# A graph network on one core: where the last stores are issued, and the order inside some neighbour groups

## The chip, the cores and the metric

The kernel runs on one core of one Trainium2 chip. A core has five engines that run side by side and meet at semaphores: TensorE (PE, matrix products; its weight loads are listed as PEld), VectorE (DVE), ScalarE (ACT), GpSimd (POOL) and SyncE (SP, which here only issues transfers). SBUF holds the working data, PSUM takes what PE writes. Transfers (DMAs) are issued from the queues of SP, ACT and POOL.

The metric is the device time of one execution in microseconds. Three runs of the kernel before gave 1960.7, 1963.19 and 1964.54; the median is 1963.19.

## The reference

There are 128 graphs of 128 nodes with 256 features, all float32, and an adjacency matrix for each. Two layers follow each other, both with a layer norm, a ReLU and a residual:

```
h = relu(layernorm(x))
s = h @ w_se.T + b_se                          # three features per node
A = exp(-|s_n - s_m|^2) * adj                  # distances, masked
msg = relu(h @ w_msg.T + b_msg)
x_nmp = A @ msg                                # the neighbours' messages
x_conv = relu(h + bn2(conv17(relu(bn1(conv1(h))))))   # along the nodes
x = x + gru([x_conv, x_nmp], h)                # gates r, z and n

h = relu(layernorm(x))                         # second layer: nodes 0..24 only
for g in five groups of nodes:
    h1 = relu(normadj_g @ (h_g @ W1[g]) + b1[g])
    fused[:, nodes of g] += softmax(w)[g] * relu(normadj_g @ (h1 @ W2[g]) + b2[g])
x = x + fused
```

## The kernel before, in words

**Tiling.** Four graphs make a group (`GB = 4`), so there are 32 groups, numbered 0 to 31. The convolution of 17 taps is done by a Fourier transform of 80 points, in two batches of 16 groups.

**Stages.** Layer A (`stage_a`) normalises, makes the first product and transforms. Layer B (`stage_b`) multiplies, for each of 40 frequencies, the transformed data by transformed weights, which POOL adds up beforehand (tiles `xs` and `wf`, L544 and L545). So the sequence is A, B for the first batch, A, B for the second. Then layer C (`stage_c`) transforms back and computes the gates for all groups, while the second layer (`rows`, `prepare`, `pair`) follows behind it for the nodes below 25.

**Neighbour groups.** Beside A, B and the start of C runs a lane of 32 programs, `early(q)`, one for each group. Each loads the group's data (two DMAs on SP, for the next group ahead), runs `neighbours`, and stores the result from POOL (`xmd`, L709). `neighbours` has these steps:
- pse: sixteen small matmuls (L647), four ACT instructions into `ef` (L651), one DVE product into `lr` (L654)
- two messages: for each, eight matmul instructions pm (L663), an addition of the bias on DVE (L666) and a ReLU on ACT (L668)
- the distances: a product of `lr` (L676) and a transpose of the adjacency (L678) for each graph into a tile `pd`, the exponential on ACT (L680) and the mask product on DVE (L681) into `aT`
- px, in two halves: messages times `aT` (L689), and a copy to `xm` on DVE (L691)

`pse`, `pm`, `pd` and `px` take turns in five PSUM buffers (pool `ptmp`).

**The order of the work.** The order in which instructions are given to each engine is fixed when the program is built, by a planner (`Order`, `Lane`). Each program is a generator that yields after a step a pair: what the step costs PE, and how long after it the next one should wait. The planner moves its own clock by the first number, and of the lanes whose next step is due it takes the one with the least work done by its weight. So `yield 0.9, 3.0` after the distances keeps px back by 3.0 of the planner's units unless there is nothing else to take. At the start of the first B the program waits 10 units, loads weights and waits 5 more; at the second B only 5; at the start of C a load waits 7 and another 6. In these times the neighbour lane is all that the planner has.

**The end.** `pair` of the last two blocks ends in the steps `turn`, `gather` and `fuse`. `fuse(h)` makes a weighted sum over the five groups of nodes for eight graphs (two matmuls of 512 columns, one for each half of the partitions), adds it to `x1` on DVE and stores it. Of the last block, h = 2 and h = 3, each graph has its own store of 32 KB: the eight of h = 2 all on SP, those of h = 3 on SP and ACT in turn.

Of the kernel before, what the change touches and what calls it, by code (L numbers as in the profile page):

```python
# [19 lines left out]
P = 128  # L20
GB = 4
# [189 lines left out]
def kernel(ctx: ExitStack, tc: tile.TileContext, x, adj, consts, vecs, w_se, conv1_w,  # L211
# [162 lines left out]
    brow = xf.tile([P, D], FP, name="brow")  # L374
    LATE, XA, MOM = {}, {}, {}
    A_DONE, B_DONE, G_DONE, C_DONE = set(), set(), {-1}, set()

    def take_turn(name, bufs, **kw):
        while turn:
            turn.pop().close()  # L380
        turn.append(ExitStack())
        LATE[name] = turn[-1].enter_context(
            tc.tile_pool(name=name, bufs=bufs, side="right", **kw))
# [142 lines left out]
    def stage_b(bat):  # L526
        while "wrz" not in LATE:
            yield 0.0, 0.5
        if bat == 0:
            yield 0.0, 10.0  # L530
        WF, xf = {}, LATE["xw"]

        def load_w(f):
            w = WF[f] = xf.tile([P, 2, 3, D], FP, tag="wf", name=f"wf{bat}_{f}", bufs=4)
            for k in range(2):
                nc.sync.dma_start(out=w[:, k, :2], in_=wfd[f::NF + 1, k * P:(k + 1) * P]
                                  .rearrange("s p o -> p s o"))

        XS = {}

        def add(f):

            XS[f] = xf.tile([P, 2, P], FP, tag="xs", name=f"xs{bat}_{f}", bufs=2)
            nc.gpsimd.tensor_tensor(XS[f], X[:, :, 2 * f], X[:, :, 2 * f + 1], ALU.add)  # L544
            nc.gpsimd.tensor_tensor(WF[f][:, :, 2], WF[f][:, :, 0], WF[f][:, :, 1], ALU.add)  # L545

        def product(ps, xk, f, s):

            for k in range(2):
                nc.tensor.matmul(ps, xk(k), WF[f][:, k, s], start=(k == 0), stop=(k == 1))  # L550

        for f in range(3):
            load_w(f)
        yield 0.0, 5.0
        late = None
        for f in range(NF + 1):
            if f + 3 <= NF:
                load_w(f + 3)
            if f < NF:
                add(f + 1)  # L560
            if f >= NF - 6 and f % 3 == 0 and bat + 1 < NBAT:
                n = (bat + 1) * BQ + (f - NF + 6) // 3
                XA[n] = LATE["xe"].tile([P, 4, D], FP, name=f"xa{n}")
                load_x(XA[n], n)
            n = (bat + 1) * BQ
            if f == NF - 3 and n in XA:
                MOM[n] = moments(XA[n], "a")
            if f == NF - 1 and n in XA:
                normalize(XA[n], XA[n], *MOM[n])
            y = xf.tile([P, 2, D], FP, tag="y", name=f"y{bat}_{f}")  # L570
            pa = pgat.tile([P, 2, D], FP, tag="gat", name=f"pa{bat}_{f}")
            for s in range(2):
                product(pa[:, s], lambda k: X[:, k, 2 * f + (s if f == 0 else 1 - s)], f, s)
            if f == 0:
                nc.vector.tensor_copy(y, pa)
            else:
                pb = ptmp.tile([P, D], FP, tag="tmp", name=f"pb{bat}_{f}")
                xs = XS.pop(f)
                product(pb, lambda k: xs[:, k], f, 2)
                kk = xf.tile([P, D], FP, tag="kk", name=f"kk{bat}_{f}", bufs=2)  # L580
                nc.scalar.activation(kk, pb, AF.Copy)  # L581
                nc.vector.scalar_tensor_tensor(y, pa, 2.0, kk[:, None].to_broadcast([P, 2, D]),  # L582
                                               op0=ALU.mult, op1=ALU.subtract)
            WF.pop(f)
            if late is not None:
                nc.gpsimd.dma_start(out=yd[bat][:, 2 * f - 2:2 * f], in_=late)
            late = y
            yield 1.7 if f == 0 else 2.6, 1.0
        nc.gpsimd.dma_start(out=yd[bat][:, F - 2:F], in_=late)
        B_DONE.add(bat)  # L590
# [49 lines left out]
    def neighbours(q, hT, ad, xm):  # L640


        bmsg = LATE["bmsg"] if q else bm0
        pse = ptmp.tile([P, 512], FP, tag="tmp", name=f"pse{q}")
        for k in range(2):
            for j in range(GB):
                nc.tensor.matmul(pse[j * WIDE:(j + 1) * WIDE, :N], wse9[:, k],  # L647
                                 hT[:, k, j * N:(j + 1) * N], start=(k == 0), stop=(k == 1))
        ef = LATE["fr"].tile([P, 4, N], FP, tag="ef", name=f"ef{q}")
        for i in range(4):  # L650
            nc.scalar.activation(ef[:, i], pse[:, :N], AF.Identity, scale=emb[:, i:i + 1],  # L651
                                 bias=embb[:, i:i + 1])
        lr = LATE["fr"].tile([P, 2, N], FP, tag="lr", name=f"lr{q}")
        nc.vector.tensor_tensor(lr, ef[:, 0::2], ef[:, 1::2], ALU.mult)  # L654
        yield 0.5, 0.0

        msgs = []
        for h in range(2):
            pm = ptmp.tile([P, 2, D], FP, tag="tmp", name=f"pm{q}_{h}")
            for i in range(2):  # L660
                j = 2 * h + i
                for k in range(2):
                    nc.tensor.matmul(pm[:, i], hT[:, k, j * N:(j + 1) * N], LATE["wmsg"][:, k],  # L663
                                     start=(k == 0), stop=(k == 1))
            msg = LATE["fr"].tile([P, 2, D], FP, tag=f"msg{h}", name=f"msg{q}_{h}")
            nc.vector.tensor_tensor(  # L666
                msg, pm, bmsg[:, None, :].to_broadcast([P, 2, D]), ALU.add)
            nc.scalar.activation(msg, msg, AF.Relu)  # L668
            msgs.append(msg)
            yield 1.75, 0.0  # L670

        pds = [ptmp.tile([P, 2, N], FP, tag="tmp", name=f"pd{q}_{j}") for j in range(GB)]
        aT = LATE["fr"].tile([P, GB, N], FP, tag="aT", name=f"aT{q}")
        for j in range(GB):
            rows = slice(j * WIDE, (j + 1) * WIDE)
            nc.tensor.matmul(pds[j][:, 0], lr[rows, 0], lr[rows, 1], start=True, stop=True)  # L676
        for j in range(GB):
            nc.tensor.transpose(pds[j][:, 1], ad[:, j], ident)  # L678
        for j in range(GB):
            nc.scalar.activation(aT[:, j], pds[j][:, 0], AF.Exp)  # L680
            nc.vector.tensor_mul(aT[:, j], aT[:, j], pds[j][:, 1])  # L681
        yield 0.9, 3.0


        for h in range(2):
            px = ptmp.tile([P, 2, 2, N], FP, tag="tmp", name=f"px{q}_{h}")
            for i in range(2):
                for dc in range(2):
                    nc.tensor.matmul(px[:, dc, i], msgs[h][:, i, dc * P:(dc + 1) * P],  # L689
                                     aT[:, 2 * h + i], start=True, stop=True)  # L690
            nc.vector.tensor_copy(xm[:, :, h * 256:(h + 1) * 256],  # L691
                                  px.rearrange("p d i n -> p d (i n)"))
            yield 0.9, 0.0
# [411 lines left out]
    def pair(pr):  # L1105
# [93 lines left out]
        def fuse(h):  # L1199
            zt, blk = hz[:, h % 3], b0 + h // 2  # L1200
            x1 = X1[blk][:, 2 * (h % 2):2 * (h % 2) + 2]
            pf = ptmp.tile([P, 2, D], FP, tag="tmp", name=f"pfu{pr}_{h}")
            for s in range(2):
                nc.tensor.matmul(pf[s * 2 * WIDE:(s + 1) * 2 * WIDE], s2w, zt[:, :, s],
                                 start=True, stop=True)
            nc.vector.tensor_add(x1, x1, pf)
            for i in range(2):
                g0 = (b0 * QS + 2 * h + i) * GB
                if blk < NBLK - 1:
                    nc.gpsimd.dma_start(out=out[g0:g0 + GB, :WIDE], in_=x1[:, i])  # L1210
                    continue
                for j in range(GB):
                    eng = nc.scalar if h % 2 and j % 2 else nc.sync
                    eng.dma_start(out=out[g0 + j, :WIDE], in_=x1[j * WIDE:(j + 1) * WIDE, i])

        tail = [(turn, 0), (turn, 1), (turn, 2), (turn, 3), (gather, 0), (turn, 4), (turn, 5),
# [25 lines left out]
    for bat, (during_a, during_b) in enumerate(((0.66, 0.5), (0.2, 0.65))):  # L1242
        if bat:
            take_turn("ab", 2, reuse_waits="tile")
        begin = Lane([stage_a(q) for q in range(bat * BQ, (bat + 1) * BQ)], ahead=3)
        beside.weight = during_a
        order.run(begin, beside, *[gates] * bat, until=begin)
        take_turn("xw", 3, reuse_waits="tile")
        products = Lane([stage_b(bat)])
        beside.weight = during_b  # L1250
        order.run(products, beside, *[gates] * bat, until=products)
    turn.pop().close()
    lab.close()
    LATE["co"] = ctx.enter_context(
# [52 lines left out]
```

## Time and profile before

| what | value |
|---|---|
| median of three runs | 1963.19 us |
| profiled execution, its own time | 1960.66 us |
| its span (first to last instruction) | 1958.9 us |
| mean granted clock of TensorE | 0.999 |
| share of the chain that ended last on PE | 83% |
| layer A and B with both batches | to about 657 us |
| neighbour groups | 161 to 801 us |
| layer C | from 671 us |
| last addition of the final sum | 1949.84 to 1950.53 us |

The profile comes from one execution. A row such as "177.43 2.05 PE L689 MATMUL px<-aT,msg ... x16 [0.97 <-DVE aT L681]" says that sixteen instructions of line 689 began at 177.43 us, took 2.05 us together, and that the engine had stood idle for 0.97 us before them until DVE wrote `aT`. The chain of waits is followed back from the last instruction: at each step to what released it.

### The profile page before, as it was taken

How to read it: one execution, taken by the hardware profiler on the slowest of the kernel's cores; microseconds unless marked ns; L12 is line 12 of the kernel's file. 1: busy time of each engine (PE TensorE's matmuls, PEld its weight loads, DVE VectorE, ACT ScalarE, POOL GpSimd, SP SyncE). 2: the span in 40 equal slices, each digit the busy share in tenths (PEclk: the TensorE clock that was granted, in tenths of full speed). 3: DMA queues.
4: the chain of work that ended last, by engine and by line, in shares of the span. 5: the costliest groups of instructions: out<-in, count | busy, mean ns of one | idle time of the engine just before them, and what ended most of it. 6: DMA issues, size and time to landing. Idle time of an engine off the chain costs nothing.

```text
span 1958.9 us, 32171 instructions
## 1 busy us (share of the span) xinstructions
PE 1925.5 (98%) x12048; PEld 1591.1 (81%) x12048; DVE 1341.2 (68%) x2965; ACT 670.8 (34%) x1504; POOL 656.7 (34%) x899
## 2 busy tenths in 40 slices
PE   9999999999999999999999999999999999999997
PEld 6668888889888888887888787888877788887865
DVE  6775445786443576796883886885788787588852
ACT  4664222445223334322223332232332223223233
POOL 3452666332565201332321333231133222114220
PEclk9999999999999999999999999999999999999999
DMA  9988878744778744633433344254344334334232
GB/s 217 308 276 271 272 252 286 218 142 172 251 255 260 213 114 132 188 95 84 112 95 97 96 108 112 79 134 97 92 115 101 89 101 112 100 90 120 63 70 68
DMA packets 180982, 296.66 MB, mean 151 GB/s; under 512 B 28326, under 2 KB 131947, under 8 KB 180571
## 3 DMA queue, kind: packets, MB, share of 16 engines
q1 hardware_dynamic: 134874, 162.20, 28.9%
q0 software_dynamic: 44800, 131.66, 23.8%
q8 instruction: 95, 1.56, 0.3%
q10 hardware_dynamic: 1152, 0.74, 0.1%
q14 instruction: 61, 0.49, 0.1%
HBM read 197.97 MB, written 109.05 MB: 157 GB/s over the span
## 4 chain that ended last, share of the span: by engine, by line
PE 83%; DVE 11%; DMA 2%; ACT 1%; issue 1%; SPq 1%; POOL 0%; DVEq 0%; ACTq 0%; POOLq 0%
PE p L776 37%; PE pa L550 7%; PE pm L663 5%; PE pz L1150 5%; PE ph L1138 5%; PE pc L429 4%; PE pb L550 3%; PE pf L444 3%; PE px L689 3%; PE pi L733 2%; PE pw L496 1%; DMA xa<-in_x 1%; PE ph L418 1%; PE py L1122 1%; DVE xc L742 1%
## 5 line engine op out<-in xcount | busy, mean ns | idle before, releaser
L958 POOL DMA_DIRECT2D x1d<-xt x128 | 101.2, 815 | 403.6 <-DVE xt L956 390.5
L582 DVE SCALAR_TENSOR_TENSOR y<-pa,kk 128x512 f32<-128x512 f32 x78 | 53.8, 690 | 151.4 <-ACT kk L581 151.4
L858 POOL DMA_DIRECT2D xt<-in_x x128 | 100.6, 793 | 161.3 <-DMA x1d<-xt 148.1
L550 PE MATMUL pa<-wf,X 128*128 128x256 f32 x640 | 152.2, 381 | 0.0
L776 PE MATMUL p<-th,wrz 128*128 128x256 f32 x512 | 134.2, 384 | 0.0
L776 PE MATMUL p<-tm,wrz 128*128 128x256 f32 x512 | 131.4, 379 | 0.0
L776 PE MATMUL p<-tc,wrz 128*128 128x256 f32 x512 | 131.4, 379 | 0.0
L550 PEld LDWEIGHTS pa<-wf,X 128*128 128x128 f32 x640 | 118.1, 190 | 16.2 <-issue 2.0
L429 PE MATMUL pc<-c1w,hTa 128*128 128x256 f32 x512 | 120.9, 382 | 2.8 <-DVE X L450 1.7
L663 PE MATMUL pm<-wmsg,hT 128*128 128x256 f32 x512 | 121.5, 382 | 0.0
L776 PEld LDWEIGHTS p<-th,wrz 128*128 128x128 f32 x512 | 94.7, 190 | 19.1 <-issue 6.6
L429 PEld LDWEIGHTS pc<-c1w,hTa 128*128 128x128 f32 x512 | 93.6, 190 | 20.1 <-DVE h L432 4.8
L776 PEld LDWEIGHTS p<-tc,wrz 128*128 128x128 f32 x512 | 97.2, 190 | 13.5 <-issue 0.5
L663 PEld LDWEIGHTS pm<-wmsg,hT 128*128 128x128 f32 x512 | 95.8, 190 | 15.2 <-ACT kk L581 1.4
L776 PEld LDWEIGHTS p<-tm,wrz 128*128 128x128 f32 x512 | 97.3, 190 | 13.2
L745 ACT ACTIVATE xc<-xc,t_bn 128x256 f32<-128x256 f32 x128 | 58.1, 501 | 145.3 <-DVE xc L742 145.3
L776 PE MATMUL p<-hTc,wrz 128*128 128x256 f32 x384 | 99.7, 382 | 1.3 <-DVE z L850 1.2
L776 PE MATMUL p<-xc,wrz 128*128 128x256 f32 x384 | 98.6, 379 | 0.0
L776 PE MATMUL p<-xm,wrz 128*128 128x256 f32 x384 | 98.5, 379 | 0.0
L545 POOL TENSOR_TENSOR wf<-wf 128x512 f32<-128x512 f32 x78 | 98.5, 1263 | 0.0
L1138 PE MATMUL ph<-yz,w 128*128 128x400 f32 (+3 forms) x448 | 96.6, 369 | 1.8 <-DVE yz L1125 1.8
L1150 PE MATMUL pz<-hz,w 128*128 128x400 f32 (+3 forms) x448 | 95.7, 368 | 0.5 <-DVE yz L1152 0.5
(213 smaller groups left out, 4329.5 us busy)
## 6 DMA issues: line engine op xcount, KB each, us to landing
wf<-wfd SPq DMA_DIRECT2D x160, 256.0 KB
wfd<-ws POOLq DMA_DIRECT2D x64, 320.0 KB, 9.3
yd<-y POOLq DMA_DIRECT2D x80, 256.0 KB, 4.4
yt<-yd SPq DMA_DIRECT2D x64, 320.0 KB
xa<-in_x SPq DMA_DIRECT2D x128, 128.0 KB
hTd<-hTa POOLq DMA_DIRECT2D x32, 512.0 KB, 6.5
hT<-hTd SPq DMA_DIRECT2D x32, 512.0 KB
xmd<-xnmp POOLq DMA_DIRECT2D x32, 512.0 KB, 6.0
```

The source lines that it names most:

```text
L429: nc.tensor.matmul(pc[:, i], hT[:, k, (2 * h + i) * N:(2 * h + i + 1) * N], c1w[:, k], start=(k == 0), stop=(k == 1))
L444: nc.tensor.matmul(pf[:, i, :F * NB], h1[:, 2 * h + i, k * P:(k + 1) * P], fwd, start=True, stop=True)
L545: nc.gpsimd.tensor_tensor(WF[f][:, :, 2], WF[f][:, :, 0], WF[f][:, :, 1], ALU.add)
L550: nc.tensor.matmul(ps, xk(k), WF[f][:, k, s], start=(k == 0), stop=(k == 1))
L663: nc.tensor.matmul(pm[:, i], hT[:, k, j * N:(j + 1) * N], LATE["wmsg"][:, k], start=(k == 0), stop=(k == 1))
L689: nc.tensor.matmul(px[:, dc, i], msgs[h][:, i, dc * P:(dc + 1) * P], aT[:, 2 * h + i], start=True, stop=True)
L745: nc.scalar.activation(xc[:, co, s], xc[:, co, s], AF.Relu, bias=sft["bn2"][:, co:co + 1])
L776: nc.tensor.matmul(ps[:, m], w[:, i, k, m * P:(m + 1) * P], factor(i, x, t), start=first and j == 0, stop=last and j == len(n) - 1, skip_g ...
L858: nc.gpsimd.dma_start(out=xt[a * WIDE:(a + 1) * WIDE].rearrange("p b d c -> p (b d) c"), in_=slices(x[q * GB:(q + 1) * GB])[a])
L958: nc.gpsimd.dma_start(out=slices(x1d[q])[a], in_=xt[a * WIDE:(a + 1) * WIDE].rearrange("p b d c -> p (b d) c"))
L1138: nc.tensor.matmul(ph, w1[:, k, m * P:(m + 1) * P], yz[:, k, s:s + nb, o:o + n], start=(k == 0), stop=(k == 1))
L1150: nc.tensor.matmul(pz, w2[:, g, m, cc * P:(cc + 1) * P], hs[i][:, m], start=(m == 0), stop=(m == 3))
```

## The change

There are two edits. In `neighbours` a flag, read after the first step, chooses between two orders. Where it is down the order is the old one. Where it is up, the distances are given out after the first message and before the second, with the transposes ahead of the products, and the step of its own (`yield 0.9, 3.0`) is left out, so that px follows the second message. The flag is set when a pass of layer A is finished, taken down at every frequency of layer B, and set again before layer C, where it stays up.

In `fuse` the stores and the sum of the last block are divided in another way. For h = 2 the first four graphs go out in one store on POOL; all other single stores alternate between SP and ACT. For h = 3 the sum is made in two halves of 256 columns, each with its own addition.

```diff
+    LONE = [False]
...
@@ stage_b @@
+            LONE[0] = False
             y = xf.tile([P, 2, D], FP, tag="y", name=f"y{bat}_{f}")
...
@@ neighbours @@
+        alone = LONE[0]
+
+        def distances():
+            pds = [ptmp.tile([P, 2, N], FP, tag="tmp", name=f"pd{q}_{j}") for j in range(GB)]
+            aT = LATE["fr"].tile([P, GB, N], FP, tag="aT", name=f"aT{q}")
+            if alone:
+                for j in range(GB):
+                    nc.tensor.transpose(pds[j][:, 1], ad[:, j], ident)
+            for j in range(GB):
+                rows = slice(j * WIDE, (j + 1) * WIDE)
+                nc.tensor.matmul(pds[j][:, 0], lr[rows, 0], lr[rows, 1], start=True, stop=True)
+            if not alone:
+                for j in range(GB):
+                    nc.tensor.transpose(pds[j][:, 1], ad[:, j], ident)
+            for j in range(GB):
+                nc.scalar.activation(aT[:, j], pds[j][:, 0], AF.Exp)
+                nc.vector.tensor_mul(aT[:, j], aT[:, j], pds[j][:, 1])
+            return aT
+
         msgs = []
         for h in range(2):
+            if alone and h:
+                aT = distances()
             pm = ptmp.tile([P, 2, D], FP, tag="tmp", name=f"pm{q}_{h}")
...
-        pds = [ptmp.tile([P, 2, N], FP, tag="tmp", name=f"pd{q}_{j}") for j in range(GB)]
...
-        yield 0.9, 3.0
+        if not alone:
+            aT = distances()
+            yield 0.9, 3.0
...
@@ fuse @@
-            for s in range(2):
-                nc.tensor.matmul(pf[s * 2 * WIDE:(s + 1) * 2 * WIDE], s2w, zt[:, :, s],
-                                 start=True, stop=True)
-            nc.vector.tensor_add(x1, x1, pf)
+            final = blk == NBLK - 1 and h % 2
+            for i in (slice(0, 2),) if not final else (slice(0, 1), slice(1, 2)):
+                for s in range(2):
+                    nc.tensor.matmul(pf[s * 2 * WIDE:(s + 1) * 2 * WIDE, i], s2w, zt[:, i, s],
+                                     start=True, stop=True)
+                nc.vector.tensor_add(x1[:, i], x1[:, i], pf[:, i])
             for i in range(2):
                 g0 = (b0 * QS + 2 * h + i) * GB
-                if blk < NBLK - 1:
+                if blk < NBLK - 1 or (i == 0 and not final):
                     nc.gpsimd.dma_start(out=out[g0:g0 + GB, :WIDE], in_=x1[:, i])
                     continue
                 for j in range(GB):
-                    eng = nc.scalar if h % 2 and j % 2 else nc.sync
+                    eng = nc.scalar if j % 2 else nc.sync
                     eng.dma_start(out=out[g0 + j, :WIDE], in_=x1[j * WIDE:(j + 1) * WIDE, i])
...
@@ tile_gnn_kernel @@
         order.run(begin, beside, *[gates] * bat, until=begin)
+        LONE[0] = True
         take_turn("xw", 3, reuse_waits="tile")
...
+    LONE[0] = True
     turn.pop().close()
```

## The prediction

> **What bounds the kernel now.** I read the page's busy times first, then the chain of waits, then the timeline of TensorE (PE) wherever PE stood still, and last the queues at the very end.
>
> ```profile
> PE 1925.5 (98%) x12048; PEld 1591.1 (81%) x12048; DVE 1341.2 (68%) x2965; ACT 670.8 (34%) x1504; POOL 656.7 (34%) x899
> ```
>
> PE is busy 1925.5 of 1958.9 us at a granted clock of 0.999. So 33 us in all can be won without taking matmuls away, and this change takes none away: it moves idle time of PE, and it moves the end of the span.
>
> The chain of waits shows the idle time that the first edit aims at (columns: start, us, what):
>
> ```profile
> 175.47 0.70 DVE msg L666
> ...
> 176.26 0.63 ACT msg L668
> 176.89 0.18 ACT aT L680
> ...
> 177.43 2.05 PE px L689 x16
> ```
>
> The second message's matmuls (pm) end at 175.45. After them its addition and ReLU, then the exponential and the mask product, stand between PE and px. The same groups on PE's timeline, with the other place of this kind at 663.77:
>
> ```profile
> 177.43 2.05 PE L689 MATMUL px<-aT,msg 128*128 128x128 f32 x16 [0.97 <-DVE aT L681]
> ...
> 183.54 1.89 PE L550 MATMUL pa<-wf,X 128*128 128x256 f32 x8
> ...
> 663.77 2.05 PE L689 MATMUL px<-aT,msg 128*128 128x128 f32 x16 [0.97 <-DVE aT L681]
> ```
>
> Two groups (1 and 25, by counting the pse rows) cost 0.97 us each. Group 2 stood before the first Fourier product too (183.54), but its distances fell behind that product and cost nothing. The timelines of VectorE (DVE) show what can hurt:
>
> ```profile
> 173.45 0.43 DVE L654 TENSOR_TENSOR lr<-ef 128x256 f32<-128x256 f32 x1 [1.51 <-ACT ef L651]
> ...
> 181.72 3.47 DVE L654 TENSOR_TENSOR lr<-ef 128x256 f32<-128x256 f32 x1 [1.51 <-ACT ef L651]
> ...
> 664.23 0.42 DVE L618 TENSOR_TENSOR th<-hTc 128x256 f32<-128x256 f32 x1
> ```
>
> The same lr took 0.43 us alone and 3.47 us while POOL ran its xs and wf sums (181.06 to 184.90). At the end, on the queue of SyncE (SP), with its row in the table of waits last:
>
> ```profile
> 1948.63 0.36 SPq L1214 DMA_DIRECT2D out<-x  x1
> ...
> 1953.34 0.31 SPq L1214 DMA_DIRECT2D out<-x  x1
> ...
> 1956.09 0.42 SPq L1214 DMA_DIRECT2D out<-x  x1
> ...
> SPq L1214 <- DMA out<-x: 1.6, 3, 1.2
> ```
>
> SP issues 12 of the 16 small stores, ACT four from 1950.56 on; three of SP's wait for the landing of an earlier store (1.6 us), the first from about 1952.1 to 1953.34, and the last starts at 1956.09. The span ends 2.8 us after that start.
>
> **The final stores.** Taken away: 12 issues on SP and 4 on ACT. Put in: one 128 KB store on POOL, six small ones each on SP and ACT. The last addition (0.69) starts at 1949.84, after four matmul instructions of 512 columns in 1.67 us. In halves there are eight of 256; PE must still wait for the second ReLU, so the first half can be added about 0.4 earlier and the last ends near 1950.25, for 1950.53. That 0.3 counts only if nothing later binds, and something does: the waits on landings say that from the ninth small store on a store needs an early one landed. With twelve stores, four instead of eight are behind that point. Taking the observed 1953.34 for the first of them, SP issues two in 0.46 steps, the last starts at 1953.8 and the end is 1953.8 + 2.8 = 1956.6: a gain of 2.3. If the early ones land at once, SP's last starts near 1951.2, but then the POOL store ends it: 1948.63 + 5.0 (median issue to landing of the four such stores, 4.1 to 5.9) = 1953.6, plus about 1.2 of closing work = 1954.8; a gain of 4.1. If the fifth POOL store delays the early small ones by 1.6 (a fifth of the 7.9 us from the first POOL store's issue at 1944.84 to the last one's landing, 1947.76 + 5.0), the gain is 0.7. POOL, ACT and SP have nothing else queued. I take 2.0, near the row.
>
> The Trainium skill, "DMA: Bandwidth & Descriptors", section "Issuing engines are not separate DMA queues", speaks against this part: more issuing engines save only the issuing time. By it the five or six issues that leave SP would be worth about 2.4 us (six by 0.4) and nothing of the landing waits; the rows above have those waits besides.
>
> **Which groups are alone.** The flag is read after a group's first step. It is up from the end of a layer A pass to the first product, and in all of layer C. By the planner's own costs a group shrinks from 6.7 plus 3.0 of delay to 5.8, so more fits into the 15 units (10 + 5, first pass), 5 (second) and about 13 (7 + 6, layer C) that pass before the main lane's first product. Ahead of the first product come all of groups 1 and 2 and half of group 3; ahead of the second, all of group 15; ahead of C, one whole group more. The work on PE is only put earlier. On SP the loads of group 3 now go before the first wf loads, which then start near 176.5 instead of 166.9; their product comes near 189, so 1.5 MB has about 12 us. On POOL group 2's store goes before the first sums; they are done about 3.5 us after group 2's px, and the product that reads them stands behind group 3's second message, about 7 us after it.
>
> **What an alone group costs.** PE: pse 0.57, pm 1.83, transposes and distances 1.1, pm 1.83, px. The exponentials and mask products are now under the second message: there the 0.97 goes. What is late next is that message: by the chain it is ready 1.5 us after its matmuls (175.45 to 176.89 and a hand-over), and the first half of px covers only 0.9. The second half of px waits about 0.6, with hand-overs 0.65. Nothing else can step between, since no other lane is ready, and everything behind on PE waits too.
>
> Sum over the places, in PE idle time:
> - First product: group 1, 0.65 for 0.97: -0.3. Group 2 had cover, now +0.65. Group 3's lr meets POOL's sums, and its distances are now asked for after one message and one product instead of after both messages: between 0 and 1.2, I take 0.9, by the 3.47 row. Together +1.25.
> - Second product: group 15 hid its distances behind two products, now +0.65 (0.5 to 1.0).
> - Layer C: 0.97 before; now two groups of 0.65, and the eight sums of C (L618, 664.23 to 667.24, 3.0 us of DVE) fall between a group's first message and its mask products or lr: 0 to 2.2, I take 1.2, in the middle, because the place depends on the planner's phase. Together +1.5 (-0.3 to +2.5).
> - Inside C: PE idles 2.0 us between 671 and 850 (179.00 less 176.99 in the table of windows), where five groups are woven in. Two of them now run earlier: 2/5 of it, -0.8. The ends: all 2.0 goes, or each of four groups pays 0.65 (+2.6).
> - End: -2.0 (-4.1 to -0.7).
>
> Sum: 1.25 + 0.65 + 1.5 - 0.8 - 2.0 = +0.6 us. The profiled execution took 1960.66 (span 1958.9 and 1.8 around it), 2.5 below the median 1963.19 of three runs; on the median the forecast is **1963.8**.
>
> For the lr row the Trainium skill, "SBUF — State Buffer", section "Who interferes with whom", has a VectorE operation with two SBUF inputs block fully until the reading GpSimd operation is done. By that rule as written lr would wait out one sum (at most 1.26 us, the longest POOL row there); the 3.47 row waited out the whole run of four, and with one sum group 3 would pay nothing and the total would be -0.3.
>
> **The rivals.** A difference of 0.2% (3.9 us: below 1959.3, above 1967.1) is about what a measurement of this kernel can tell from no change.
> - *Faster.* The second message hides: px waits only for hand-overs. Groups 1 and 25 give back 0.97 each, the three others pay 0.1 each, lr meets no sums, C gives 0.8, the end 2.0: -4.4, 1958.8; with the end's full 4.1 it is 1956.7. For it: the two 0.97 rows are exactly this pause. Against it: the 0.70 and 0.63 of msg in the chain, longer than half a px.
> - *Slower.* In C the alone groups pay at the second px, on a DVE that is 74% busy there (132.56 of 179.00), so that the message's addition queues: 1.0 (the longest wait of px on aT) by four groups, +4.0 in place of -0.8: +5.4, 1968.6. It decides from three such groups on. Against it: in C other matmuls can stand between the two halves of px, and did for group 27 to 30.
> - *The end does not move.* The fifth POOL store holds up the small ones, and the ring of landings still sets the end: -0.7 for -2.0, 1965.1. For it: the POOL stores' 5.0 us. It stays within 0.2%.
>
> **Chances.** Forecast 0.38, end not moving 0.12: within 0.2% 0.50. Faster 0.26, slower 0.24; the bounds of C and of the end make both sides possible. The likeliest case by itself spans 1961 to 1966; the range goes to the other cases, 1957.5 to 1968, leaving about 1 in 10 on each side.
>
> **What would show it.** Right: in groups 1 and 2 px splits into two halves with a wait of 0.6 between them, released by ACT's message, and no wait at the first half; group 2's px ahead of the first pa; 12 small stores and one more on POOL; the last small store starting near 1953.8. Wrong: px without a gap (faster), new gaps of px on msg or aT between 690 and 790 (slower), a last store after 1955 (end not moving). A layer C reordered so far that gaps past 850 change by more than 2 us would upset the whole sum.

## The result, and the profile after

The changed kernel takes 1975.72 us (median of six runs, 1972.73 to 1981.6). The kernel before, run beside it, takes 1962.19 (six runs, 1960.41 to 1965.22). The ratio is 1.0064, with a 95% interval of 1.0048 to 1.0081: **slower by 13.5 us**. The forecast was 1963.8, a rise of 0.6, and its range ended at 1968.

The profiled execution took 1979.52 us. Its span is 1977.7 us, 18.8 longer than the 1958.9 of before, and its granted clock is 0.994 for 0.999. The busy times from the page:

```profile
PE 1933.8 (98%) x12052; PEld 1599.9 (81%) x12052; DVE 1354.3 (68%) x2966; ACT 662.5 (34%) x1498; POOL 657.7 (33%) x900
```

PE does the same matrix work as before (the four instructions more are the halves of the last sum), yet it is busy 8.3 us longer. So the 18.8 us are two things: 8.3 of busy time and 10.6 of idle time. The busy time goes with the clock: in some stretches the profile shows a granted clock of 0.5, called half clock here. This table adds up PE's gaps by place. The last column is PE's busy time inside the stretches at half clock, halved, since that work would have taken half as long at full clock; without it PE is busy 1924.9 us, for 1925.5 before.

| place (time in the trace after) | idle before | idle after | difference | half clock adds |
|---|---|---|---|---|
| start, to the first neighbour group (0 to 165) | 6.05 | 9.51 | +3.5 | 2.6 |
| groups ahead of the first product (165 to 202) | 1.31 | 2.76 | +1.45 | 0 |
| second layer A pass (355 to 513) | 3.62 | 6.95 | +3.3 | 4.7 |
| groups ahead of the second product (513 to 530) | 0.00 | 2.93 | +2.9 | 0 |
| groups ahead of layer C (688 to 714) | 0.97 | 2.50 | +1.5 | 1.7 |
| layer C with groups woven in (714 to 839) | 2.01 | 2.33 | +0.3 | 0 |
| the rest, to the last matmul | 10.32 | 10.37 | +0.1 | 0 |
| last matmul to the end of the span | 9.08 | 6.54 | -2.5 | 0 |

The sum is 10.6 idle and about 9.0 at half clock, 19.6 for the 18.8 seen. The start runs the same instructions in both kernels, and its idle time lies between 4.0 and 11.0 us over the profiles of this study. Without its 6.1 us the table gives +13.5, which is the difference of the medians. That they agree so well is luck: the table compares one execution with one, and the execution of before has less half clock than most. Its granted clock is 0.999, where the executions of before that were timed beside the experiments have 0.994 to 0.999 and a median of 0.997.

**Ahead of the first product.** PE's timeline of after (start, us, instruction, and in brackets the idle time before it with its releaser):

```profile
180.41 1.05 PE L702 MATMUL px<-aT,msg 128*128 128x128 f32 x8
182.08 1.16 PE L702 MATMUL px<-aT,msg 128*128 128x128 f32 x8 [0.61 <-ACT msg L691]
...
190.06 1.16 PE L702 MATMUL px<-aT,msg 128*128 128x128 f32 x8 [0.61 <-ACT msg L691]
...
196.98 0.50 PE L669 MATMUL pd<-lr 32*128 32x128 f32 x8 [1.10 <-DVE lr L656]
```

The single pause of 0.97 ahead of px has gone. In its place px is split by 0.61 in groups 1 and 2, and group 3's distances wait 1.10 for their lr.

**The second layer A pass.** PE's longest waits in that stretch, of after (total us, times, longest):

```profile
PE ph L419 <- DVE xa L282: 1.8, 1, 1.8
PE pd L669 <- DVE h L433: 1.3, 1, 1.3
PE ph L419 <- ACT hTa L421: 1.1, 1, 1.1
PE pf L445 <- DVE msg L689: 1.1, 1, 1.1
PE pf L445 <- DVE aT L675: 0.7, 1, 0.7
```

and of before in the same pass, where there are five in all, for eight, and none is longer than 1.2:

```profile
PE pd L676 <- DVE h L432: 1.2, 1, 1.2
PE ph L418 <- DVE aT L681: 0.9, 1, 0.9
PE pd L676 <- ACT hTa L420: 0.6, 1, 0.6
```

No line of layer A was edited, and no group that starts in this pass is alone.

**The clock.** Windows of after (columns: the window; its length; busy time and instructions of PE, PEld, DVE, ACT and POOL; PE's granted clock; DMA share; GB/s):

```profile
374.70:378.10 3.40, 1.64 (x11) 1.18 (x9) 3.33 (x13) 1.29 (x5) 1.20 (x1) 1.00 0.87 237
378.10:381.60 3.50, 3.50 (x17) 3.50 (x16) 3.40 (x12) 2.07 (x4) 0.00 (x0) 0.51 1.05 286
405.50:408.90 3.40, 1.83 (x11) 1.10 (x11) 3.40 (x9) 0.63 (x1) 0.59 (x1) 1.00 0.17 69
408.90:412.30 3.40, 2.50 (x9) 1.99 (x10) 0.66 (x2) 2.08 (x6) 0.96 (x2) 0.50 0.00 0
412.30:415.70 3.40, 3.40 (x13) 3.13 (x13) 1.25 (x5) 0.88 (x4) 1.43 (x1) 0.50 0.92 284
702.40:705.80 3.40, 1.56 (x10) 0.97 (x9) 3.31 (x10) 0.63 (x1) 0.00 (x0) 1.00 1.04 342
705.80:709.20 3.40, 3.35 (x25) 2.71 (x26) 0.72 (x2) 0.13 (x2) 0.25 (x1) 0.51 1.09 228
```

Three times a window in which PE was busy about half of 3.40 us (1.64, 1.83, 1.56) is followed by one or two windows at half clock. In each of the three DVE is busy nearly all the time (3.31 to 3.40), and most of the waits there are for it. Such a pause is paid twice, once as idle time and again as work at half speed. In the profile of before no such stretch lies within the working part.

**Ahead of the second product.** Timelines of DVE, PE and POOL of after:

```profile
515.61 3.47 DVE L656 TENSOR_TENSOR lr<-ef 128x256 f32<-128x256 f32 x1 [1.51 <-ACT ef L653]
519.13 0.50 PE L669 MATMUL pd<-lr 32*128 32x128 f32 x8 [2.83 <-DVE lr L656]
514.94 0.74 POOL L545 TENSOR_TENSOR xs<-X 128x256 f32<-128x256 f32 x1
515.63 1.27 POOL L546 TENSOR_TENSOR wf<-wf 128x512 f32<-128x512 f32 x1
516.86 0.72 POOL L545 TENSOR_TENSOR xs<-X 128x256 f32<-128x256 f32 x1
517.54 1.25 POOL L546 TENSOR_TENSOR wf<-wf 128x512 f32<-128x512 f32 x1
```

The product lr takes 3.47 us and ends at 519.08, after the last of four POOL sums (518.79), and PE waits 2.83 for it.

**The end.** The last small store of SP, PE's last matmuls, and SP's waits there, of after:

```profile
1974.81 0.32 SPq L1229 DMA_DIRECT2D out<-x  x1
1970.54 0.65 PE L1219 MATMUL pfu<-hz,s2w 128*64 128x256 f32 x4 [0.51 <-DVE x L1221]
SPq L1229 <- DMA out<-x: 1.4, 2, 0.8
```

The second half of the last sum waits 0.51 for the addition of the first half, and its matmuls take 1.89 us where the four longer ones of before took 1.67. So the matmuls end 0.7 later, and the stores end 2.5 earlier relative to them: 1.8 net. Two waits on landings remain (1.4 us) where there were three (1.6).

### The profile page after: what moved, and what is told of

Its sections match the earlier page's. It is cut to its first block, busy times and chain, and to the rows that moved or that the text cites. A ratio compares the mean times of both kernels' runs of the same rounds, so it can differ in the third digit from the quotient of the medians.

```text
span 1977.7 us, 32176 instructions
## 1 busy us (share of the span) xinstructions
PE 1933.8 (98%) x12052; PEld 1599.9 (81%) x12052; DVE 1354.3 (68%) x2966; ACT 662.5 (34%) x1498; POOL 657.7 (33%) x900
## 3 DMA queue, kind: packets, MB, share of 16 engines
q8 instruction: 95, 1.56, 0.3%
## 4 chain that ended last, share of the span: by engine, by line
PE 83%; DVE 11%; DMA 3%; issue 1%; ACT 1%; SPq 0%; DVEq 0%; POOL 0%; ACTq 0%
PE p L789 37%; PE pa L551 7%; PE pm L686 5%; PE pz L1163 5%; PE ph L1151 5%; PE pc L430 4%; PE pb L551 3%; PE pf L445 3%; PE px L702 3%; PE pi L746 2%; PE pw L497 1%; PE ph L419 1%; PE py L1135 1%; PE pse L649 1%; DMA xa<-in_x 1%
## 5 line engine op out<-in xcount | busy, mean ns | idle before, releaser
L1165 DVE COPY yz<-pz 128x400 f32<-128x400 f32 (+3 forms) x56 | 23.0, 410 | 109.0 <-PE pz L1163 109.0
```

## The experiments

Two theories stood against each other. The **pause theory** (the expectations call it the wait theory) takes the prediction's own terms and only resizes them: each alone group, that is each group in the new order, pays inside itself. The **order theory** says that the loss comes from the steps being shorter for the planner, which puts the neighbour lane a group further ahead and so meets layer A, POOL's sums and layer C at other moments. A third question was what the half clock follows. Ratios are to the kernel before on the same chip, with 95% intervals.

### One place at a time

The end alone, with no group ever alone:

```
-        alone = LONE[0]
+        alone = False
```

> The change's end alone: stores on three queues and the last sum in halves, neighbour groups as before. Both theories of the neighbour edit expect the same here: -2.6 us, the distance from the last matmul's end to the span's end going from 9.1 to 6.5 us as in the changed kernel, so about 1959.6 us. Against it stands that the end is off the path in another run: then 1962.

The same kernel timed again, more often:

> The change's end alone once more, with more rounds, because its first timing (ratio 1.0002) left out the 2.0 us that the profiles show between the last matmul and the span's end. End theory: ratio 0.999, about -2 us, with the interval reaching to the first timing's. If the gain is lost elsewhere in time: 1.000 or more again, and the profile must then show where between the products and the end the 2.0 us are given back.

The groups alone, with the final stores and the final sum as before:

```
-            final = blk == NBLK - 1 and h % 2
+            final = False
...
-                if blk < NBLK - 1 or (i == 0 and not final):
+                if blk < NBLK - 1:
...
-                    eng = nc.scalar if j % 2 else nc.sync
+                    eng = nc.scalar if h % 2 and j % 2 else nc.sync
```

> The neighbour edit alone, stores and last sum as before. Both theories: the 13.5 us of the whole change plus the 2.6 that the end gives back, so about +16 us, 1978. If the two edits hinder each other, less than +13.

And from this kernel, the flag raised at one place only: `LONE[0] = bat == 0` ahead of the products and `False` at layer C for the first, `bat == 1` and `False` for the second, `False` and `True` for the third.

> The neighbour edit with the flag up only at the first pass (before the first product), stores as before. Order theory: the second layer A pass is already moved by it, so +8 us or more, with stretches at half the granted clock between 370 and 415 us. Wait theory: only the places of groups 1 to 3 pay, +1.3 us, and the clock stays at 0.999.

> The flag up only at the second pass, stores as before. Only what follows about 485 us can differ. In the changed kernel the group there lost 2.8 us because lr met POOL's sums; here the group ahead of the second product is another one, whose lr was ready 0.6 long in the kernel before. Order theory (POOL's sums start when the store ahead of them is out, so the phase decides): +0.6 to +1 us from the second message's wait, no stretch at half clock, 1963 to 1965. Wait theory with starvation at every such place: +3 to +5.

> The flag up only in layer C, stores as before. By the sums of the prediction +0.7 (lead +1.5, inside C -0.8): 1963 to 1965. By the changed kernel's gaps +1.5 in the lead, +0.4 inside and one stretch of 3.4 us at half the clock: +3.6. Gaps of at most 2 us at one place and a clock of 0.999 speak for the first, a half-clock stretch after a window with more than half its time idle for the second.

Measured:

| kernel | median us | before | ratio |
|---|---|---|---|
| end alone | 1964.39 | 1964.24 | 1.0002 [0.9991, 1.0013] |
| end alone, again | 1963.58 | 1964.52 | 0.9995 [0.9980, 1.0010] |
| all groups alone, old end | 1981.12 | 1964.24 | 1.0092 [1.0074, 1.0111] |
| first product only | 1975.73 | 1964.24 | 1.0063 [1.0044, 1.0083] |
| second product only | 1961.86 | 1962.53 | 1.0004 [0.9988, 1.0021] |
| layer C only | 1964.14 | 1962.53 | 1.0006 [0.9991, 1.0022] |

**Most of the loss comes with the flag before the first product**: 0.0063 of the 0.0092 that all alone groups cost with the same old end, both within some 0.002. Yet PE pays only 1.45 us more at that place. In the trace of that kernel the second layer A pass idles 6.94 us (3.62 before), has a stretch of 6.83 us at half clock from 407.4, and shows the very waits of the changed kernel. Ahead of layer C, where none of its groups is alone, it idles 3.32. PE's timeline there:

```profile
694.68 3.40 PE L702 MATMUL px<-aT,msg 128*128 128x128 f32 x16 [2.89 <-DVE aT L675]
```

With the flag at the second product only, the lead there (the groups ahead of the stage) idles 0.70 (one px split by 0.61), close to the 0.65 of the prediction. With the flag before the first product only, PE does not idle there at all, though the shifted group's lr takes 3.48 us (from 514.55): its distances stand behind the first matmuls of that product. So the 2.93 of the changed kernel needs both, a group that arrives there at another moment and the new order inside it.

Ahead of layer C it is the other way round. With the flag at layer C only, where nothing earlier is shifted, PE idles the same 2.50 us as in the changed kernel: 0.61 for one group's message, and these two waits of the next group:

```profile
674.00 1.16 PE L702 MATMUL px<-aT,msg 128*128 128x128 f32 x8 [1.13 <-DVE aT L675]
675.92 1.16 PE L702 MATMUL px<-aT,msg 128*128 128x128 f32 x8 [0.76 <-ACT msg L691]
```

So that idle time is the price of alone groups at layer C, and not of the shift. No half clock followed it in this kernel.

The end alone shows its gain in the profile (6.57 us after the last matmul for 9.08, less 0.7 for the split sum, so 1.8; the nine other traces with the old end have 8.7 to 9.0). But the medians do not resolve it: its two intervals reach from 2.0 per mille faster to 1.3 slower. The profile of the second timing has 7.37 us at the end, and a wait of 5.04 us at 166 that no edit explains. Between all groups alone and the changed kernel the ratios differ by 5.5 us, more than the end's 1.8, but both intervals are some 3.5 us wide on either side.

### The order or the group

If alone groups still give the planner the old step, with no work in it, all other work keeps its place, and only the inside of the alone groups is new:

```
-        if not alone:
-            aT = distances()
-            yield 0.9, 3.0
+        if not alone:
+            aT = distances()
+        yield 0.9, 3.0
```

> The neighbour edit alone, but an alone group keeps an empty step of 0.9 with the delay of 3.0 after its second message, so that the planner gives out everything else in the old order (SP and POOL lists unchanged). Order theory: the loss comes from the moved order of what follows, the second layer A pass above all (PE gaps there 6.9 us for 3.6, granted clock at half for two stretches), so it vanishes: -2 to +2 us against before, and granted clock 0.998 or more. Wait theory: the loss is the wait of an alone group for its second message and for lr; it stays, +5 us or more.

The opposite, from the kernel with the flag at the first product only: every group keeps its old inner order (both messages, then the distances), and only the planner's steps get short.

```
-        alone = LONE[0]
+        alone, short = False, LONE[0]
...
-            if alone and h:
-                aT = distances()
...
             msgs.append(msg)
+            if short and h:
+                aT = distances()
             yield 1.75, 0.0
-        if not alone:
+        if not short:
             aT = distances()
             yield 0.9, 3.0
```

> No group changes its inside: the distances stay behind both messages everywhere. Only the planner's bookkeeping is that of the neighbour edit, in the first pass alone: the groups ahead of the first product cost it 5.8 in place of 6.7 and 3.0 of delay. From group 4 on every engine's order is that of first_only. Order theory: the loss of first_only stays: waits of 6.9 us in the second layer A pass and about 3 us ahead of layer C, at least one stretch at half clock after them, +8 to +12 us. Wait theory: the loss came from inside groups 1 to 3, so at most +1 (one more pause of 0.97).

Measured: with the old steps kept 1970.12, ratio 1.0032 [1.0016, 1.0047]; with short steps and the old inner order 1975.11, ratio 1.0056 [1.0034, 1.0078]. The second reproduces nearly all of the 1.0063 of the flag at the first product without one group that is alone. The second layer A pass, by windows over the whole pass, of before:

```profile
341.00:482.00 141.00, 137.38 (x902) 123.73 (x901) 106.23 (x290) 68.91 (x156) 43.22 (x51) 1.00 0.54 173
```

of the changed kernel:

```profile
355.00:513.00 158.00, 151.05 (x971) 134.82 (x970) 110.61 (x302) 73.69 (x168) 43.77 (x52) 0.97 0.53 170
```

and of the kernel with the old steps kept:

```profile
343.00:484.00 141.00, 137.39 (x888) 123.68 (x888) 106.18 (x290) 67.74 (x153) 43.16 (x51) 0.99 0.53 168
```

(The pass is longer in the changed kernel because more of a group falls into it; what compares is length less PE's busy time: 3.6, 6.9 and 3.6 us.) With the short steps and the old inner order it is 6.9 again, with these waits:

```profile
PE ph L419 <- DVE xa L282: 1.8, 1, 1.8
PE pd L669 <- DVE h L433: 1.3, 1, 1.3
```

the same rows as in the changed kernel. Ahead of layer C the same trace gives PE's wait, by DVE's timeline:

```profile
691.75 0.42 DVE L620 TENSOR_TENSOR tm<-tm,xm 128x256 f32<-128x256 f32 x1
692.09 0.87 DVE L675 TENSOR_TENSOR aT<-aT,pd 128x128 f32<-128x128 f32 x4
```

The mask products stand behind the last of the eight sums of layer C (L620, from 689.16 on), and px waits 2.88 for them. **In the second layer A pass the order theory holds and the pause theory fails**: the shift alone makes the loss there. It also makes a wait of its own ahead of layer C, but in the changed kernel, with alone groups there, other waits stand in its place, those of the flag at layer C.

With the old steps kept PE idles in the pass as before, and the lead of C falls from 0.97 to 0.61, the first gain of the new inner order. But 1.0032 is still a loss, where the order theory expected none: what goes on inside the groups has a price too. Its trace shows it at group 2, 2.83 us of waiting for lr and then 3.41 us at half clock, and inside layer C, where PE idles 3.79 us for 2.01 before: the second pm of an alone group waits up to 1.8 for DVE, and 3.41 us at half clock follow (from 777.4). A third such stretch in this trace, from 367.8 in the second pass, follows waits that before has too.

### The wait for lr

Group 2 only, with the old steps kept (`alone = q == 2`):

> Only group 2 takes the new order, and the empty step keeps the planner's order of all else; stores as before. Starvation theory: lr takes about 3.5 us beside POOL's sums, PE waits 2.8 us for it and, if that lies in one window of the clock, loses 1.7 us more at half the clock: +3 to +4.5. Message theory: only the second message's wait counts, and it is covered by the product that follows: 0 to +0.7.

The same, with POOL's sums of the frequencies 1 and 2 of the first batch replaced by fills (the kernel leaves these sums out, so two frequencies are not computed):

```
+            if bat == 0 and f < 3:
+                nc.gpsimd.memset(XS[f], 0.0)
+                nc.gpsimd.memset(WF[f][:, :, 2], 0.0)
+                return
             nc.gpsimd.tensor_tensor(XS[f], X[:, :, 2 * f], X[:, :, 2 * f + 1], ALU.add)
```

> As the one before, but POOL fills xs and the third part of wf with zeros for frequencies 1 and 2 of the first batch instead of adding (those sums are left out, so two frequencies of the first batch are not computed). A fill only writes. Starvation theory (two readers of SBUF meet): lr is back at 0.43 us and PE's wait at group 2 under 0.5. If any POOL work of that length holds lr up, lr stays above 2 us and the wait stays.

Measured: group 2 alone costs 1967.9, ratio 1.0029 [1.0014, 1.0045]. DVE's and PE's timelines and two windows of it:

```profile
186.41 3.47 DVE L656 TENSOR_TENSOR lr<-ef 128x256 f32<-128x256 f32 x1 [1.51 <-ACT ef L653]
189.93 0.50 PE L669 MATMUL pd<-lr 32*128 32x128 f32 x8 [2.83 <-DVE lr L656]
```

```profile
188.30:191.70 3.40, 1.67 (x13) 1.37 (x14) 2.48 (x4) 1.13 (x5) 1.28 (x2) 1.00 0.00 0
191.70:195.10 3.40, 3.40 (x9) 2.66 (x8) 1.27 (x4) 0.80 (x2) 0.00 (x0) 0.50 0.02 5
```

With fills in place of sums, the same two rows:

```profile
187.33 0.42 DVE L660 TENSOR_TENSOR lr<-ef 128x256 f32<-128x256 f32 x1 [1.51 <-ACT ef L657]
187.95 0.50 PE L673 MATMUL pd<-lr 32*128 32x128 f32 x8
```

POOL's four instructions still lie around lr (186.63 to 188.14), but lr takes 0.42 and PE does not wait. So it is the sums that hold lr, and not that POOL is busy. The one run took 1967.02 in all; its start idled 10.6 us and had 6.83 us at half clock, so its total says nothing about group 2. One group's change of inner order costs 5.4 us by the medians (1967.9 less 1962.53; the interval reaches from 2.7 to 8.8): 2.83 of wait and 1.7 at half clock are 4.5 of it.

### The half clock

Into the kernel before, longer and longer pauses of PE were put in layer C, far from any neighbour group, by repeated copies of `xc` on DVE:

```
         xc = XC.pop(q)
+        for _ in range({8: 2, 12: 3, 16: 4, 20: 6, 24: 9}.get(q, 0)):
+            nc.vector.tensor_copy(xc, xc)
```

> The kernel before with 2, 3, 4, 6 and 9 copies of xc onto itself on DVE ahead of groups 8, 12, 16, 20 and 24 of layer C, so that PE idles there for growing times. Clock theory: a stretch of 3.4 us (or two) at half the granted clock follows each place where a window of 3.4 us is less than about half busy, so behind the pauses of about 2 us and more and not behind those under 1.5; each such stretch adds 1.7 us of PE time. If the clock does not follow PE's idle time, the granted clock stays at 1 there and PE's busy time does not grow.

Measured: 1983.46 us. The five pauses came out as 1.06, 2.33, 2.44, 3.72 and 6.07 us. The last three brought half clock, for 3.41, 3.41 and 6.83 us (the longest stretch began within its pause); the first two did not. Windows around the second, third and fourth:

```profile
1155.40:1158.80 3.40, 1.73 (x8) 1.55 (x9) 3.26 (x8) 0.56 (x1) 0.00 (x0) 1.00 0.01 2
1158.80:1162.20 3.40, 3.40 (x18) 2.99 (x17) 3.14 (x5) 0.16 (x2) 0.00 (x0) 1.00 0.00 0
1295.30:1298.70 3.40, 0.96 (x5) 0.54 (x4) 3.26 (x6) 0.69 (x2) 0.00 (x0) 1.00 0.36 141
1298.70:1302.10 3.40, 3.40 (x9) 2.67 (x8) 3.23 (x10) 0.60 (x1) 0.93 (x1) 0.51 0.00 0
1459.20:1462.60 3.40, 0.43 (x2) 0.41 (x3) 3.20 (x5) 0.00 (x0) 0.00 (x0) 1.00 0.69 228
1462.60:1466.00 3.40, 3.40 (x10) 2.69 (x9) 3.29 (x7) 0.60 (x1) 0.00 (x0) 0.50 0.00 0
```

2.33 and 2.44 us of pause differ only by where they fall: the first is split over two windows and leaves PE 1.73 busy in one, the second falls into one and leaves 0.96. So the length of a pause doesn't decide alone; how much of it falls into one window counts too, and the windows' phase differs from run to run.

### A version that keeps what is good

The new inner order only in the two groups whose px waited 0.97 (1 and 25), the old steps for the planner, and the new end:

```
-        alone = LONE[0]
+        alone = q in (1, 25)
...
-            yield 0.9, 3.0
+        yield 0.9, 3.0
```

> The change's end, and the new order inside groups 1 and 25 alone (those that paused 0.97 before), with the empty step that keeps the planner's order. By both theories each gives 0.97 - 0.61 = 0.36 back and the end 2.0: -2.7 us, 1960. If the end's gain is not real in time, -0.7, which is no difference.

Measured: 1960.0 us (twelve runs, 1956.65 to 1963.87) against 1963.72 (nineteen runs), ratio 0.9982 [0.9968, 0.9995]: **faster than the kernel before** by 1.8 per mille, with an interval that just leaves out no change. Its profile has a span of 1957.8 us, a clock of 0.999, and px on PE's timeline split by 0.61 in both groups:

```profile
179.63 1.16 PE L702 MATMUL px<-aT,msg 128*128 128x128 f32 x8 [0.61 <-ACT msg L691]
...
665.64 1.16 PE L702 MATMUL px<-aT,msg 128*128 128x128 f32 x8 [0.61 <-ACT msg L691]
```

That is 0.36 less idle time at each place and 6.50 for 9.08 us at the end, less the 0.7 of the split sum: 2.6 in the trace, for 3.7 by the medians.

## Why the prediction was wrong

**What held.** The inside of an alone group is as told: the exponentials and mask products hide under the second message, and px splits with a wait of 0.61 for ACT's message (0.65 forecast). The first product's lead lost 1.45 (1.25 forecast), with group 3's lr among it (1.10; 0.9 forecast). The lead of layer C lost 1.5 idle, as forecast, and by the mechanism forecast: px waits for the message, and for mask products behind the eight sums of C; the kernel with the flag only there loses the same. (By its own terms the range given for this sum starts at +0.3, not at -0.3.) The end gained 1.8 in the trace, near the 2.0 of the forecast, though in another way: the last store starts 3.6 us after the last matmul, sooner than the 4.0 worked out, and the split sum costs 0.7 that was not in the sum, mostly because the second half's matmuls wait for the first half's addition: counted from the start of the last sum, the last addition ends 0.5 later, where the forecast had it 0.3 earlier.

**The step that failed is "The work on PE is only put earlier."** It looked at the three places where the flag is up and took all that lies between as unmoved. But putting a group earlier shifts the whole lane against layer A. In the second pass the five waits above, four of them for DVE, stand where shorter ones stood: +3.3 idle, for which the sum had nothing. The kernel with short steps and no alone group shows the same waits, so the shift is the cause. Why just these moments are bad ones is not shown. A full DVE isn't enough: in the trace of before it is as busy in the two windows from 361.0 on (3.33 of 3.40 us each), and PE still works 2.23 and 2.93 us in them.

**The clock was taken as 0.999 throughout.** Nothing in the forecast let a pause of PE cost more than itself. By the table above that missed 4.7 us in the second pass and 1.7 ahead of layer C. Of this only one part comes with the shift every time: all four traces with it (the changed kernel, all groups alone, the flag at the first product, short steps) have 6.83 us at half clock from 405 to 409 on, worth 2.6 to 3.0, and none of the ten others has. The stretch from 378 is in two of the four (from 374.9 with short steps), and 3.41 us at half clock also stand in three of the ten second passes that keep the order of before. The stretch at layer C is missing with all groups alone, after the same waits.

**The term of the second product** (+0.65, between 0.5 and 1.0) was right for the place as it stood, as the kernel with the flag only there shows (0.70). In the changed kernel it is 2.93: the shifted group's lr falls beside POOL's sums, and in the new order PE waits for it. The forecast had this price, the 3.47 row, and used it for group 3 only.

**Inside C** nothing came back: +0.3 for -0.8. The row that says why is PE's longest wait there:

```profile
PE pm L686 <- DVE aT L675: 2.3, 1, 2.3
```

An alone group asks for its second message's buffer right after its four tiles of distances, and pm and pd share five buffers, so pm waits until a mask product has let one go. (That the buffer is what pm waits for is argued from the row and the pool, not tried.) DVE isn't what holds the mask products up. ACT's and DVE's timelines of after:

```profile
779.76 0.91 ACT L804 ACTIVATE r<-r,brz 128x256 f32<-128x256 f32 x2 [2.11 <-DVE r L880]
780.68 1.28 ACT L674 ACT_TABLE_LOAD   x1
782.29 0.88 DVE L675 TENSOR_TENSOR aT<-aT,pd 128x128 f32<-128x128 f32 x4 [2.23 <-ACT aT L674]
```

DVE itself waits 2.23 us for ACT, where the group's exponentials stand behind an activation of the gates (L804) and a table load of 1.28 us. The forecast looked for this group's price at px only.

Beside the table's total of +13.5 stands the forecast +0.6. Of the difference of 12.9, the second pass is 8.0 (3.3 and 4.7), the second product's lead 2.3, the half clock at C 1.7 and the inside of C 1.1: 13.1 together, with small terms that nearly cancel.

**The rivals.** The slower side came true, with none of its rival's mechanism: that rival placed the loss at px within layer C, where no px of the changed kernel waits and PE idles only 0.3 more than before. The last condition named in the forecast, a reordering that changes gaps outside the places looked at, was the right worry, but it was put past 850 us, and it happened between 355 and 513.

## What to carry to other kernels

When the order of the work is planned from step costs, an edit of one step's cost moves every later meeting of its lane with the others: keep the planner's steps as they were while the inside is changed, and measure the two apart. Before an operation with two SBUF operands on DVE is put where its result is waited for, look at what POOL reads at that moment. And a pause of PE of some 2 us may have to be paid again as a stretch at half clock, so a few gaps that fall close together can cost more than their sum.

## What the runs showed of the hardware

**The half clock.** Before the last matmul it comes in stretches of 3.41 or 6.83 us, on a grid of 3.41 us whose phase differs between runs. It followed windows with PE busy 1.56 to 1.83 of 3.40 us in the changed kernel, so gaps that add up to 1.6 us in one window were enough. The limit isn't sharp. In the same trace the windows from 514.7 (1.60 busy) and 780.9 (1.67) were followed by full clock, as was the ladder's 1.73. In layer C, where PE works on narrow matrices, a window with 2.50 busy at 778.2 was followed by half clock in the kernel with the new end alone, while one with 2.50 at 774.0 was not in the kernel before. Seven of the fourteen traces have a stretch that begins between 776 and 787, four of them with layer C's work in the order of before. What decides there stays open. The phase makes luck: in the second pass the same wait of 1.16 us left PE 1.77 busy in a window of the kernel with the old steps kept, and half clock followed. In the kernel before the wait (1.17) lay in a window with 2.23 busy, and none did. The Trainium skill, "TensorE: Matmul & The Clock Gate", section "Part 1: The HAM clock gate", tells of a free-running window of 3413 ns after which an idle PE gets half its clock; the stretches agree with that length. Its rule of no idle gap above about 3.4 us isn't strict enough by these traces: of the pauses of 1.8 and 1.3 us in the second pass 1.6 us fell into the window from 405.5, and 6.83 us at half clock followed.

**DVE behind POOL.** Two-operand lr took 0.42 us beside fills and 3.47 beside four sums on POOL (3.46 and 3.47 in the traces of before, of the changed kernel, of group 2 alone and of the old steps kept): it ends only once the last sum has ended. The Trainium skill, "SBUF — State Buffer", section "Who interferes with whom", says that a two-input DVE operation contends with POOL operations that read, not with those that only write. Both halves agree with these rows. It speaks of waiting for one instruction (at most 1.27 us here), and the rows show that DVE did not get its turn between four back to back.

**The start.** In code that no edit touches, PE idled from 4.0 to 11.0 us before the first neighbour group. In seven of the fourteen traces 3.5 to 6.1 us of it are one gap between 111 and 137 us. With the half clock after it, this may be much of the spread of several us between runs of one kernel; neither that nor its cause was tried.
